# Layer 1's last norm: mean and gamma folded into the projection, squares of centered sums on ScalarE, residual added by TensorE

## The chip, the core and the metric

The kernel runs on one core of a Trainium2 chip, in one launch. The metric is the device time of that core in microseconds. Engines are named as in the profile: PE (TensorE, matmuls), DVE (VectorE), ACT (ScalarE), POOL (GpSimd) and SP (which issues the DMAs).

## The reference, cut to what matters

The input is 8 images of 192 channels and 56 x 56 pixels, in fp32. Four layers follow each other, each added to its input after a group norm. Layer 0 is an involution; layers 1 to 3 are state-space (Mamba) layers. The change is in layer 1 alone:

```python
xn = _ln(xf, ln_gamma, ln_beta)                                    # over 192 channels
xs = three slices of 64 channels, handled as three sequences
y  = _mamba(xs, ...) + skip_scale * xs
y  = y put together to 192 channels
y  = _ln(y, ln_gamma, ln_beta)                                     # the last norm
y  = y @ proj_W.T + proj_b
x  = x + y
# _ln: mu = mean(x); xc = x - mu; var = mean(xc * xc); xc * rsqrt(var + 1e-5) * g + b
```

## The kernel before

**Chunks and units.** The 3136 pixels of an image are cut into 7 chunks of 448 columns (`T`), so layer 1 has 56 chunks. A chunk is three jobs, one for each slice of 64 channels (kinds 0, 1, 2). A job is 16 units: 4 blocks of 128 inner channels times 4 groups of state rows (`nd` = 4, `NQ` = 4). The first `ssm_layer` loop runs over all units, in an order written out by hand (`manual_schedule`): each engine executes its instructions in the program's order.

**A unit** has two scans on DVE (L796), one for each half of a tile `uhg` of 128 x 4 x 448. A scan reads its decay factors from the PSUM tile `da` of that half, which ACT fills with two exponentials (`decays`, L764) as soon as the unit before has finished its scan of the same half. The scan's input is a product (L792 on DVE with a row that TensorE spread over the partitions, L752; or L785 on POOL), made one unit ahead by DVE and two ahead by POOL. After the scans ACT keeps the last column (L800, `carry`); POOL multiplies `uhg` by a row of C two units later (`readout`, L805); TensorE adds up over the states three units later (`reduce`, L814, with L811 at the start of a block); DVE multiplies the finished block by its gate (`gated`, L830). Tile `uhg` has 9 buffers. `nothing` (L820) issues matmuls with a zero weight to TensorE where the plan has little for it.

**Background steps.** All other work is made of `Step`s: matmuls, and a rest that another engine does with their result. `Steps.run` first flushes the pending rests down to `left`, then issues the step's matmuls and leaves its rest pending. So a rest is issued when a later step's `left` asks for it; `pause` (left 9) flushes nothing, `flushed` (left 0) flushes all. Matmul results lie in the PSUM pool `mm`, which has two buffers. A job has 32 places, two for a unit: an even place lies before the unit's first scan, an odd one between the first and the second. `places` deals the steps of a stretch out over its places by their costs.

**The last norm of a chunk** (`finish`) runs while the next chunk's kind-0 job is scanned, in places 18 to 31 (units 9 to 15), ahead of four gate matmul steps (L1098). It consists of `layer_norm_steps` on the tile `y` of 64 x 3 x 448:

- average: three matmuls with the constant matrix `lavg` (all 1/192), L557; its rest subtracts the mean on DVE (L563) and squares on ACT (L565, tile `sq`);
- variance: three matmuls of `lavg` with the squares, L557; its rest is logarithm and exponential on ACT (L569, L570);
- scale on DVE (L574), then the affine step on ACT, three activations (L579).

Then come two projections of three matmuls each (L1060) with a rest on DVE that adds bias and residual (L1066), and the leave step: a DMA of the chunk to the stream in HBM and two batch statistics on DVE (L298). On an image's last chunk two small group norm steps follow. In a chunk that is not an image's last, the planner puts the average at place 18, its flush at 19, the variance at 21, its flush at 22, the scale at 23, the affine step at 24, the projections at 25 and 27, and the leave step at 29. On an image's last chunk leave is at 28.

The first norm of the following chunk uses the same `layer_norm_steps` and is not changed. Weights of a layer are loaded by `load_weights` at the layer's start. In the profile an fp32 matmul shows as two records.

Of the kernel before, what the change touches and what calls it, by code (L numbers as in the profile page):

```python
# [10 lines left out]
F32 = mybir.dt.float32  # L11
BF16 = mybir.dt.bfloat16
AF = mybir.ActivationFunctionType
ALU = mybir.AluOpType
# [4 lines left out]
CP = 96  # L19
# [67 lines left out]
def conv_mamba_stack(ctx: ExitStack, tc: tile.TileContext, a, out):  # L87
# [9 lines left out]
    def const(shape, src=None, eng=None, dt=F32):  # L97
        n_const[0] += 1
        t = cst.tile(shape, dt, tag=f"k{n_const[0]}", name=f"k{n_const[0]}")
        if src is not None:  # L100
            (eng or nc.sync).dma_start(out=t, in_=src)
        return t

    def mm_tile():
        return banks.mm.tile([128, 512], F32, tag="mm", name="mm")
# [83 lines left out]
    g64 = const([64, 3], per_channel("L1_gamma", 64))  # L189
    b64 = const([64, 3], per_channel("L1_beta", 64))  # L190
    skip = const([64, 1], a["L1_skip"].partition_broadcast(64))
    skip_d = const([64, 64])
    nc.vector.tensor_scalar_mul(skip_d, ident[:64, :64], skip[:, 0:1])

# [51 lines left out]
    def load_weights(pool, w):  # L246

        pre, nd = w.pre, w.nd

        def load(tag, shape, src, eng=nc.sync):  # L250
            t = pool.tile(shape, F32, tag=tag, name=tag)
            eng.dma_start(out=t, in_=src)
            return t


        w.xproj = pool.tile([128, nd, w.rank + 2 * NS], F32, tag="w_x", name="w_x")
        xproj = a[pre + "x_proj"].rearrange("(j p) m -> p j m", p=128)
        nc.sync.dma_start(out=w.xproj[:, :, : 2 * NS], in_=xproj[:, :, w.rank :])
        nc.sync.dma_start(out=w.xproj[:, :, 2 * NS :], in_=xproj[:, :, : w.rank])
        w.dtw = pool.tile([2 * NS + w.rank, nd * 128], F32, tag="w_dt", name="w_dt")  # L260
        nc.vector.memset(w.dtw[: 2 * NS], 0.0)
        nc.sync.dma_start(out=w.dtw[2 * NS :], in_=a[pre + "dt_proj"])
        if nd == 4:
            w.inb = None
            w.outw = load("w_out", [128, 4, 64], a[pre + "out_proj"].rearrange("(j p) m -> p j m", p=128))
            w.projw = load("w_proj", [64, 3, CH], a[pre + "proj"].rearrange("(i p) o -> p i o", p=64))
        else:
            w.inw = load("w_in", [CP, NCT, 768], a[pre + "in_proj"].rearrange("(t p) m -> p t m", p=CP))
            w.inb = None
            if pre == "L2_":  # L270
                merge_embedding(pool, w)
            w.outw = load("w_out", [128, 3, CH], a[pre + "out_proj"].rearrange("(j p) m -> p j m", p=128))
            w.convd = pool.tile([128, nd, 4, 128], F32, tag="w_conv", name="w_conv")
            for j in range(nd):
                for k in range(4):
                    nc.vector.tensor_scalar_mul(w.convd[:, j, k, :], ident, w.convw[:, j, k : k + 1])
        w.dd = pool.tile([128, nd, 128], F32, tag="w_d", name="w_d")
        for j in range(nd):
            nc.vector.tensor_scalar_mul(w.dd[:, j, :], ident, w.dvec[:, j : j + 1])
# [739 lines left out]
    def mamba_jobs(pool, w):  # L1019
        jobs = []  # L1020
        chunks = Chunks(pool, 1)
        cks = chunks.all
        for ck in cks:
            c = ck.c

            def norm(c=c, ck=ck):
                def gnorm():
                    ck.xn = chunks.normalized(ck, None, 1)

                def slices():  # L1030

                    xn = ck.xn
                    xs = pool.tile([128, 3, T + 3], F32, tag="xs", name="xs", bufs=2)
                    ck.xs = xs
                    if c == 0:
                        nc.gpsimd.memset(xs[:64, :, 0:2], 0.0)
                        nc.gpsimd.memset(xs[64:, :, 0:3], 0.0)
                    else:
                        before = cks[ck.place - 1].xs
                        nc.scalar.copy(xs[:64, :, 0:2], before[:64, :, T : T + 2])  # L1040
                        nc.scalar.copy(xs[64:, :, 0:3], before[64:, :, T : T + 3])
                    for h in range(2):
                        for p0, p1, i, src in ((0, 64, 0, xn[0:64, 0, :]), (0, 32, 1, xn[64:96, 0, :]),
                                               (32, 64, 1, xn[0:32, 1, :]), (0, 64, 2, xn[32:96, 1, :])):
                            nc.sync.dma_start(out=xs[64 * h + p0 : 64 * h + p1, i, 2 + h : T + 2 + h], in_=src)

                return (
                    [Step(None, gnorm, 2)] + layer_norm_steps(pool, lambda: ck.xn, CP, NCT, g96, b96)
                    + [Step(None, slices, 2)]
                )  # L1050

            ck.norm = norm

            def finish(c=c, ck=ck):
                pps = {}

                def proj(t):
                    pps[t] = mm_tile()
                    for i in range(3):
                        nc.tensor.matmul(  # L1060
                            pps[t][:CP, :T], lhsT=w.projw[:, i, t * CP : (t + 1) * CP], rhs=ck.y[:, i, :],
                            start=(i == 0), stop=(i == 2),
                        )

                def add(t):
                    nc.vector.scalar_tensor_tensor(  # L1066
                        ck.x[:, t, :], pps[t][:CP, :T], w.projb[:, t : t + 1], ck.x[:, t, :], ALU.add, ALU.add
                    )

                return layer_norm_steps(pool, lambda: ck.y, 64, 3, g64, b64) + [  # L1070
                    Step(lambda t=t: proj(t), lambda t=t: add(t), 1, 3) for t in range(NCT)
                ] + [pause()] + chunks.leave_steps(ck)

            for i in range(3):

                def prepare(u, *beside, i=i, ck=ck, norm=norm):
                    def conv_mm(j):
                        pm = mm_tile()
                        for k in range(2):
                            nc.tensor.matmul(  # L1080
                                pm[:, :T], lhsT=w.inconv[:, k, j * 128 : (j + 1) * 128],
                                rhs=ck.xs[:, i, 2 - 2 * k : 2 - 2 * k + T], start=(k == 0), stop=(k == 1),
                            )
                        return pm

                    convs, *others, stores = project_steps(pool, w, u, conv_mm, 2, *beside)
                    if i == 0:
                        stores = stores + [Step(None, lambda: chunks.fetch_next(ck), 2)]
                        if ck.place == 0:
                            convs = norm() + convs  # L1090
                    return convs, *others, stores

                def gates(u, i=i, ck=ck):
                    normed = cks[ck.place + 1].norm() if i == 2 and ck.place + 1 < len(cks) else []

                    def z_mm(j):
                        pm = mm_tile()
                        nc.tensor.matmul(  # L1098
                            pm[:, :T], lhsT=w.inz[:, j * 128 : (j + 1) * 128], rhs=ck.xs[:64, i, 2 : T + 2], start=True, stop=True
                        )  # L1100
                        return pm

                    return normed + gate_steps(pool, w, u, z_mm, 1)

                def after(u, i=i, ck=ck, finish=finish):
                    def out_proj():
                        u.ps = mm_tile()
                        nc.tensor.matmul(u.ps[:64, :T], lhsT=skip_d, rhs=ck.xs[:64, i, 2 : T + 2], start=True, stop=False)
                        for j in range(4):
                            nc.tensor.matmul(u.ps[:64, :T], lhsT=w.outw[:, j, :], rhs=u.zs[:, j, :], start=False, stop=(j == 3))  # L1110

                    def leave():
                        if i == 0:
                            ck.y = pool.tile([64, 3, T], F32, tag="y", name="y")
                        nc.scalar.copy(ck.y[:, i, :], u.ps[:64, :T])

                    def fetch():
                        if i == 2:
                            chunks.fetch_again(ck)

                    return fetch, [Step(out_proj, leave, 1, 5)], finish() if i == 2 else []

                jobs.append((i, c == 0, prepare, gates, after))
        return jobs
# [165 lines left out]
```

## Time and profile before

| | us |
|---|---|
| median of 3 runs | 24391.19 (24375.81 to 24401.58) |
| the profiled execution | 24428.22 |
| its span | 24426.4 |
| first scan of layer 1 starts | 1623.88 |
| first scan of layer 2 starts | 16705.70 |
| mean granted TensorE clock | 0.84 |

The page gives each engine's busy time and share of the span. The groups give, after the count, busy microseconds in all and mean nanoseconds of one, and then the idle time of the engine just before them. The timeline gives start, length, engine, line and operation; a bracket names the idle time before it and what ended it. Durations of neighbours on an engine overlap a little, so that start to start is shorter than a duration.

### The profile page before, as it was taken

The page shows a single profiled execution, that of the slowest core. Times are in us where ns is not written, and L with a number is a line of the kernel's source. Part 1 is how long each engine was busy: PE and PEld are TensorE (multiplying, and loading weights), DVE is VectorE, ACT ScalarE, POOL GpSimd, SP SyncE. Part 2 cuts the span into 40 slices and gives each one's busy share as a digit, 9 for nine tenths or more (in the row PEclk, how much of TensorE's full clock was granted, in tenths as well). Part 3 has the DMA queues.
Part 4 walks back from the last instruction along what each step waited for, and adds up shares of the span by engine and source line. Part 5 has one row for each costly group of instructions (what it writes and reads, how often), then busy time and mean ns, then how long its engine had stood idle before and what let it go on. Part 6 is the DMA issues. An engine that isn't in the chain of part 4 may idle for free.

```text
span 24426.4 us, 238439 instructions
## 1 busy us (share of the span) xinstructions
PE 20547.5 (84%) x74445; PEld 6487.3 (27%) x74445; DVE 23026.9 (94%) x15882; ACT 17006.8 (70%) x32578; POOL 22738.4 (93%) x6775
## 2 busy tenths in 40 slices
PE   8988888888888888888888888888888887888888
PEld 2222222222222222222222222222333332333332
DVE  8989999999999999999999999997999998999999
ACT  2137777777777777777777777776777776777777
POOL 5669999999999999999999999997999998999999
PEclk9987888878887887887887887878989898999998
DMA  4433333333333333333333333333444443444443
GB/s 111 109 106 131 128 126 133 127 127 130 132 128 126 131 128 125 132 130 125 130 128 126 130 130 128 128 129 111 140 141 142 141 139 123 142 144 144 142 143 129
DMA packets 1209092, 3171.55 MB, mean 130 GB/s; under 512 B 166444, under 2 KB 470596, under 8 KB 1207688
## 3 DMA queue, kind: packets, MB, share of 16 engines
q1 hardware_dynamic: 1205016, 3155.25, 39.4%
q8 instruction: 584, 9.57, 0.2%
q14 instruction: 692, 5.67, 0.1%
q10 hardware_dynamic: 2800, 1.06, 0.0%
HBM read 2438.45 MB, written 555.55 MB: 123 GB/s over the span
## 4 chain that ended last, share of the span: by engine, by line
DVE 35%; PE 29%; ACT 14%; issue 11%; POOL 6%; DMA 5%; SPq 1%; DVEq 0%; POOLq 0%; ACTq 0%
DVE uhg L796 22%; DVE uhg L792 8%; ACT da L764 6%; PE y L814 4%; POOL uhg L805 4%; DMA rows<-bc 3%; PE mm L1110 3%; PE mm L1168 3%; PE mm L655 2%; PE mm L1080 2%; PE mm L621 2%; POOL uhg L785 2%; PE mm L429 2%; ACT dt L663 1%; PE y L820 1%
## 5 line engine op out<-in xcount | busy, mean ns | idle before, releaser
L796 DVE TENSOR_TENSOR_SCAN uhg<-da,uhg 128x898 f32<-128x898 f32 x8064 | 15913.4, 2011 | 606.9 <-ACT da L764 586.1
L805 POOL TENSOR_TENSOR uhg<-uhg,rows 128x1792 f32<-128x1792 f32 x4032 | 14730.5, 3674 | 283.6 <-ACT carry L800 267.4
L764 ACT ACTIVATE da<-rep,k 128x448 f32<-128x448 f32 x16128 | 10262.3, 636 | 1436.8 <-DVE uhg L796 1064.1
L785 POOL TENSOR_TENSOR uhg<-rep,rows 128x1792 f32<-128x1792 f32 x1795 | 7160.6, 3989 | 784.6 <-DMA rows<-bc 435.6
L814 PE MATMUL y<-uhg,k 128*32 128x448 f32 x32256 | 4516.4, 634 | 343.1 <-POOL uhg L805 341.4
L792 DVE TENSOR_TENSOR uhg<-rep,b 128x1792 f32<-128x1792 f32 x2237 | 4469.6, 1998 | 180.2 <-PE b L752 132.4
L800 ACT COPY carry<-uhg 128x4 f32<-128x4 f32 x4032 | 784.5, 195 | 3506.5 <-DVE uhg L796 3427.8
L820 PE MATMUL y<-w_d,k 128*128 128x448 f32 (+1 forms) x5280 | 2490.5, 575 | 0.0
L811 PE MATMUL y<-xc,w_d 128*128 128x448 f32 x2016 | 1533.4, 856 | 1091.2 <-DVE zs L830 1091.1
L1098 PE MATMUL mm<-xs,k 64*128 64x448 f32 x1344 | 875.4, 755 | 773.5 <-ACT zs L694 587.5
L655 PE MATMUL mm<-dbl,w_dt 36*128 36x448 f32 (+1 forms) x2016 | 1319.6, 753 | 222.4 <-ACT k L637 222.4
L814 PEld LDWEIGHTS y<-uhg,k 128*32 128x32 f32 x32256 | 679.9, 114 | 3093.6 <-issue 1935.2
L820 PEld LDWEIGHTS y<-w_d,k 128*128 128x128 f32 x5280 | 1023.1, 210 | 1645.0 <-issue 1618.3
L1136 PE MATMUL mm<-v,w_in 96*128 96x448 f32 x2688 | 1284.0, 612 | 80.3 <-ACT zs L696 36.8
L752 PE MATMUL b<-k,k 96*128 96x448 bf16 x2237 | 852.2, 381 | 446.5 <-DVE uhg L792 446.3
L1080 PE MATMUL mm<-xs,k 128*128 128x448 f32 x2688 | 1155.1, 571 | 26.3 <-ACT zs L694 11.3
L667 PE MATMUL mm<-xc,k 128*128 128x448 f32 x2016 | 1033.1, 630 | 84.4 <-DVE dt L670 84.4
L1168 PE MATMUL mm<-xin,w_conv 128*128 128x448 f32 x2688 | 1088.6, 547 | 1.4 <-ACT xin L696 0.8
L441 DVE TENSOR_TENSOR prod<-mm,shifted 128x448 f32<-128x448 f32 x1680 | 930.0, 613 | 152.5 <-PE mm L429 77.0
L811 PEld LDWEIGHTS y<-xc,w_d 128*128 128x128 f32 x2016 | 470.7, 270 | 1941.0 <-DVE zs L830 1375.2
L449 POOL TENSOR_TENSOR x<-x,one 96x448 f32<-96x448 f32 x560 | 630.7, 1134 | 265.3 <-DVE one L441 247.8
L621 PE MATMUL mm<-xc,w_x 128*36 128x448 f32 (+1 forms) x2016 | 816.4, 546 | 10.5 <-ACT xc L616 10.5
(138 smaller groups left out, 19388.1 us busy)
## 6 DMA issues: line engine op xcount, KB each, us to landing
rep<-ops SPq DMA_DIRECT2D x4032, 448.0 KB, 5.8
ops<-dt SPq DMA_DIRECT2D x1008, 448.0 KB, 3.2
rows<-bc SPq DMA_DIRECT2D x1960, 224.0 KB, 6.3
shifted<-xpad SPq DMA_DIRECT2D x672, 179.0 KB, 4.5
xg<-stream SPq DMA_DIRECT2D x168, 336.0 KB, 7.7
xr<-stream SPq DMA_DIRECT2D x168, 336.0 KB, 7.0
stream<-xr SPq DMA_DIRECT2D x112, 336.0 KB, 7.5
xs<-xg SPq DMA_DIRECT2D x224, 112.0 KB, 2.3
```

The costliest lines, as they stand in the source:

```text
L621: nc.tensor.matmul(u.ps[:nk, :T], lhsT=w.xproj[:, j, :], rhs=u.xc[:, j, :], start=(j == 0), stop=(j == nd - 1))
L655: nc.tensor.matmul(u.dps[j][:, :T], lhsT=w.dtw[:, j * 128 : (j + 1) * 128], rhs=u.dbl[:nk, :], start=True, stop=True)
L764: nc.scalar.activation(t[:, 64 + 449 * r : 512 + 449 * r], reps[k // NQ][:, 2 * h + r, 0, :], AF.Exp, scale=w.neg_a[:, j * NR + 2 * h + r, ...
L785: nc.gpsimd.tensor_mul(uhg[k][:, :, 1:], reps[k // NQ][:, :, 1, :], b)
L792: nc.vector.tensor_mul(uhg[k][:, :, 1:], reps[k // NQ][:, :, 1, :], b)
L796: nc.vector.tensor_tensor_scan(v, banks.da[h][:, 63:961], v, 0.0, ALU.mult, ALU.add)
L805: nc.gpsimd.tensor_mul(v, v, us[i].rows[1, q].unsqueeze(1).to_broadcast([128, NR, T]))
L811: nc.tensor.matmul(ys[k // NQ][:, :T], lhsT=w.dd[:, j, :], rhs=us[i].xc[:, j, :], start=True, stop=False)
L814: nc.tensor.matmul(y[32 * r : 32 * r + 32, :T], lhsT=fold, rhs=uhg[k][:, r, 1:], start=False, stop=(q == NQ - 1))
L820: nc.tensor.matmul(ys[k // NQ][:, : nd * 112], lhsT=zeros, rhs=w.dd.rearrange("p j e -> p (j e)")[:, : nd * 112], start=False, stop=False,)
L1080: nc.tensor.matmul(pm[:, :T], lhsT=w.inconv[:, k, j * 128 : (j + 1) * 128], rhs=ck.xs[:, i, 2 - 2 * k : 2 - 2 * k + T], start=(k == 0), st ...
L1168: nc.tensor.matmul(pm[:, :T], lhsT=w.convd[:, j, k, :], rhs=ck.xin[:, j, k : k + T], start=(k == 0), stop=(k == 3))
```

## The change

The mean and gamma are folded into the projection's weights when layer 1's weights are loaded (beta into the projection's bias). The variance's squares no longer come from a centered `y`: TensorE makes the centered slice `y_i - mean` in PSUM, three matmuls for each slice, and ACT squares it from there. The scale multiplies the uncentered `y`. The affine step is gone. Each projection has a fourth matmul, the identity times the residual, and its rest is an ACT activation with the bias instead of an add on DVE.

```diff
@@ constants
+    centers = const([64, 2, 64])
+    nc.vector.tensor_scalar_mul(centers[:, 1, :], lavg[:64, :64], -1.0)
+    nc.vector.tensor_add(centers[:, 0, :], ident[:64, :64], centers[:, 1, :])
@@ load_weights, layer 1
+            for t in range(NCT):
+                pm = mm_tile()
+                for i in range(3):
+                    nc.tensor.matmul(
+                        pm[:CP, :1], lhsT=w.projw[:, i, t * CP : (t + 1) * CP], rhs=b64[:, i : i + 1],
+                        start=(i == 0), stop=(i == 2),
+                    )
+                nc.vector.tensor_add(w.projb[:, t : t + 1], w.projb[:, t : t + 1], pm[:CP, :1])
+            for i in range(3):
+                nc.vector.tensor_scalar_mul(w.projw[:, i, :], w.projw[:, i, :], g64[:, i : i + 1])
+            pm = mm_tile()
+            for i in range(3):
+                nc.tensor.matmul(pm[:64, :CH], lhsT=lavg[:64, :64], rhs=w.projw[:, i, :], start=(i == 0), stop=(i == 2))
+            for i in range(3):
+                nc.vector.tensor_sub(w.projw[:, i, :], w.projw[:, i, :], pm[:64, :CH])
@@ finish
                 def proj(t):
                     pps[t] = mm_tile()
+                    nc.tensor.matmul(pps[t][:CP, :T], lhsT=ident[:CP, :CP], rhs=ck.x[:, t, :], start=True, stop=False)
                     for i in range(3):
                         nc.tensor.matmul(
                             pps[t][:CP, :T], lhsT=w.projw[:, i, t * CP : (t + 1) * CP], rhs=ck.y[:, i, :],
-                            start=(i == 0), stop=(i == 2),
+                            start=False, stop=(i == 2),
                         )
 
-                def add(t):
-                    nc.vector.scalar_tensor_tensor(
-                        ck.x[:, t, :], pps[t][:CP, :T], w.projb[:, t : t + 1], ck.x[:, t, :], ALU.add, ALU.add
-                    )
-
-                return layer_norm_steps(pool, lambda: ck.y, 64, 3, g64, b64) + [
-                    Step(lambda t=t: proj(t), lambda t=t: add(t), 1, 3) for t in range(NCT)
-                ] + [pause()] + chunks.leave_steps(ck)
+                def out(t):
+                    nc.scalar.activation(ck.x[:, t, :], pps[t][:CP, :T], AF.Identity, bias=w.projb[:, t : t + 1])
+
+                st = {}
+
+                def centered(i):
+                    st[i] = mm_tile()
+                    for k in range(3):
+                        nc.tensor.matmul(
+                            st[i][:64, :T], lhsT=centers[:, int(k != i), :], rhs=ck.y[:, k, :], start=(k == 0), stop=(k == 2)
+                        )
+
+                def square(i):
+                    if i == 0:
+                        st["sq"] = pool.tile([CP, 3, T], F32, tag="sq", name="sq")
+                    nc.scalar.activation(st["sq"][:64, i, :], st[i][:64, :T], AF.Square)
+
+                def variance():
+                    st["ps"] = mm_tile()
+                    for i in range(3):
+                        nc.tensor.matmul(
+                            st["ps"][:64, :T], lhsT=lavg[:64, :64], rhs=st["sq"][:64, i, :], start=(i == 0), stop=(i == 2)
+                        )
+
+                def rstd():
+                    pv = st["ps"]
+                    nc.scalar.activation(pv[:64, :T], pv[:64, :T], AF.Ln, bias=eps[:64, :])
+                    nc.scalar.activation(pv[:64, :T], pv[:64, :T], AF.Exp, scale=-0.5)
+
+                def scale():
+                    nc.vector.tensor_mul(ck.y, ck.y, st["ps"][:64, :T].unsqueeze(1).to_broadcast([64, 3, T]))
+
+                return [Step(lambda i=i: centered(i), lambda i=i: square(i), min(i, 1), 3) for i in range(3)] + [
+                    pause(1.0), Step(variance, rstd, 0, 3), flushed(), pause(), Step(None, scale, 0), pause(1.5),
+                ] + [Step(lambda t=t: proj(t), lambda t=t: out(t), 1, 4) for t in range(NCT)] + [pause()] + chunks.leave_steps(ck)
```

## The prediction

> **What bounds the kernel now.** I read the page first, for the engines and the chain that ended last.
>
> ```profile
> PE 20547.5 (84%) x74445; PEld 6487.3 (27%) x74445; DVE 23026.9 (94%) x15882; ACT 17006.8 (70%) x32578; POOL 22738.4 (93%) x6775
> DVE 35%; PE 29%; ACT 14%; issue 11%; POOL 6%; DMA 5%; SPq 1%; DVEq 0%; POOLq 0%; ACTq 0%
> ```
>
> VectorE and GpSimd are both nearly full, so the whole-span shares do not tell which one a saved microsecond helps. The busy time by stretch does, for layer 1 alone (columns as in the header: stretch, length, then PE, PEld, DVE, ACT, POOL busy, granted clock).
>
> ```profile
> 1700.00:16600.00 14900.00, 12429.28 (x40027) 3645.85 (x40026) 14292.43 (x8623) 10859.33 (x20855) 14568.15 (x3916) 0.80 0.38 128
> ```
>
> A chunk takes 266.24 us (the norm's scaling L574 starts at 8365.95, 8632.20 and 8898.43), so 14900 us are 56 chunks. DVE idles 608 us there, 10.9 a chunk; POOL 332, 5.9 a chunk. POOL is the fuller one, but its products lie some 10 us ahead of the scans that read them, and DVE's waits for POOL are 11 us in all. DVE's own order, with its waits for ACT and PE, sets the pace; POOL leaves room for at most 5.9 us a chunk. Next the groups of the last norm, one chunk's DVE and ACT in order of time, and the granted clock there.
>
> ```profile
> L579 ACT ACTIVATE y<-y,k,k 64x448 f32<-64x448 f32 x165 | 112.7, 746 | 0.0
> L574 DVE TENSOR_TENSOR y<-y,mm 64x1344 f32<-64x1344 f32 x55 | 84.7, 1540 | 0.0
> L563 DVE TENSOR_TENSOR y<-y,mm 64x1344 f32<-64x1344 f32 x55 | 83.6, 1521 | 0.0
> ```
>
> ```profile
> 8354.37 1.52 DVE L563 TENSOR_TENSOR y<-y,mm 64x1344 f32<-64x1344 f32 x1
> 8355.82 5.85 DVE L796 TENSOR_TENSOR_SCAN uhg<-da,uhg 128x898 f32<-128x898 f32 x3
> ...
> 8365.95 1.54 DVE L574 TENSOR_TENSOR y<-y,mm 64x1344 f32<-64x1344 f32 x1
> 8367.42 5.85 DVE L796 TENSOR_TENSOR_SCAN uhg<-da,uhg 128x898 f32<-128x898 f32 x3
> 8374.21 2.03 DVE L796 TENSOR_TENSOR_SCAN uhg<-da,uhg 128x898 f32<-128x898 f32 x1 [0.94 <-ACT da L764]
> ...
> 8381.92 1.25 DVE L1066 SCALAR_TENSOR_TENSOR xr<-mm,k,xr 96x448 f32<-96x448 f32 x2
> 8383.09 1.14 DVE L298 BATCH_NORM_STATS2 stats<-xr 96x6 f32<-96x448 f32 x2
> 8384.15 2.00 DVE L796 TENSOR_TENSOR_SCAN uhg<-da,uhg 128x898 f32<-128x898 f32 x1
> ```
>
> ```profile
> 8370.86 2.05 ACT L579 ACTIVATE y<-y,k,k 64x448 f32<-64x448 f32 x3
> 8372.82 1.29 ACT L764 ACTIVATE da<-rep,k 128x448 f32<-128x448 f32 x2
> ...
> 8382.04 1.31 ACT L764 ACTIVATE da<-rep,k 128x448 f32<-128x448 f32 x2 [0.46 <-DVE uhg L796]
> ```
>
> ```profile
> 8354.80:8358.30 3.50, 1.34 (x7) 0.45 (x4) 3.50 (x3) 2.85 (x6) 3.50 (x2) 1.00 0.00 0
> 8358.30:8361.70 3.40, 2.82 (x4) 0.45 (x2) 3.40 (x3) 2.33 (x5) 3.40 (x2) 0.50 0.00 0
> 8361.70:8365.10 3.40, 2.87 (x10) 0.70 (x10) 3.40 (x3) 3.25 (x7) 3.40 (x1) 0.50 0.18 55
> 8365.10:8368.50 3.40, 3.40 (x8) 1.33 (x5) 3.40 (x3) 0.48 (x2) 3.40 (x2) 0.50 0.93 289
> ```
>
> To be seen: DVE has no idle here but one gap, 0.94 us at 8374.21. It is caused by the three affine activations, which stand in ACT's queue ahead of the decays of that scan. And TensorE runs at half clock from 8358.3 to 8368.5, just where the variance matmuls lie; the granted clock shows the same dip at this place (mean 0.54 to 0.60 over the two units) in the other chunks.
>
> **Per chunk, along DVE.** I write the gain as a minus.
>
> Centering removed from DVE: from its start to the next scan's, 8354.37 to 8355.82, −1.45 us. The three center-and-sum products go to TensorE; nothing on DVE waits for them directly.
>
> Affine removed from ACT: the gap behind it, −0.94 us. The squares are cut in three; 448 columns read from PSUM cost ACT about 0.6 us (the Identity with bias of the same kind, L660, shows 625 ns), so no block of 2 us stands before a decay any more.
>
> Residual and bias moved off DVE: the two adds were 1.17 us (8381.92 to 8383.09). But both results stay pending until the leave step, which flushes them and queues the two statistics right behind. The statistics now wait for ACT, and ACT first runs the two decays that the scan just ended has released (8382.04, 1.24 to the next issue), a copy (0.08) and then the evictions at 0.6 each. First statistics 8384.05, second 8384.6, next scan 8385.15 instead of 8384.15: +1.0 us. Behind the waiting statistics stand the next scan and all of DVE. On images' last chunks the step falls before the other scan of the unit, with the same ACT work ahead.
>
> Scale waiting for the variance: the planner's costs put the steps, in half-unit places, as sums at 18, 19 and 20, variance at 22, its flush at 23, scale at 24; before it was average 18, variance 21, flush 22, scale 23. There is no flush between the last sum and the variance, so squares 1 and 2 enter ACT's queue together with the variance step, behind the decays of unit 11. Following the queues from 8352.45 with the rows above: scan(10,1) starts 8358.2 (the centering is gone), its decays leave ACT free at 8361.6, squares 1 and 2 end at 8362.75, variance starts 8362.8. An fp32 matmul is two records (L1060 has 672 for 336), issued 0.375 us apart at full and 0.75 at half clock; three matmuls need 2.5 us to their end at full clock (average, 8350.95, 2.47) and about 4.7 at half. Logarithm and exponential take 1.15 us. At full clock the scale may begin at 8366.55 against 8366.37 when DVE gets to it: +0.2 us. If the third sum (free to start at 8358.35, when square 0 has left its bank) and the variance both run at half clock, square 2 waits for the sum until 8363.5, the variance ends 8368.1, and the scale waits until 8369.3: +2.9 us. Between these ends I take the middle, +1.55: the clock row speaks for half speed, but the extra sums fill part of the idle stretch (PE busy 1.34 of 3.50 us) ahead of the dip.
>
> Sum: −1.45 − 0.94 + 1.0 + 1.55 = +0.16 us a chunk, times 56 = +9 us.
>
> [...]
>
> TensorE gains 8 matmuls a chunk, 16 records of 0.375, 6 us, and loses three filler matmuls of unit 11 (2.25 us). I cost these at nothing beyond the wait above: in the same stretch it idles 2.15, 1.11, 0.99, 0.74 and 3.19 us, the products' row spread (L752) is read 5 us or more after it, and the gate matmul, which waits for the adds now (3.19), will wait 1.5 us longer for the evictions but end before ACT's next gate copy. Without that cover it is up to 6 us a chunk.
>
> Once only: the folding at the start of layer 1. DVE there idles 9.45 us before the first norm; 12 small records (0.22 each by the 24 of L229 in 5.28 us), 6 of 192 columns and eight short DVE operations put about 3 us before the first average; bounds 0 and 6. The very last norm runs uncovered, three sums instead of one against no centering: +1, bounds 0 and 4. Two 64x64 operations among the constants: nothing.
>
> The profiled execution took 24428.22 us, 37 above the median of 24391.19. On it the sum is 24428 + 13; carried to the median, 24391 + 9 + 3 + 1 = 24404 us.
>
> **One thing that holds the time where it is.** The granted clock changes at multiples of 3.413 us, and a regular chunk of 266.24 us is 78.00 of them; seven chunks with an image's end (7502.20 to 9376.09) are 549.0. The chunk time is locked to these windows: an earlier or later DVE meets TensorE at another phase and is partly given back at its next waits for PE. This speaks for a result near zero.
>
> **Rivals.**
>
> Full clock: the sums keep TensorE busy enough and the stall is 0.2. Then −1.19 a chunk, −67 + 4: 24328 us. For it: of the clock's windows of 3.413 us in layer 1 that PE filled at full clock, 1370 of 1420 were followed by another at full clock. Against: the idle before the third sum remains, some 1.8 us.
>
> Half clock, the slow side: third sum and variance both at half clock, the stall on DVE before the scale is 2.9 us, +1.51 a chunk, +85 + 4: 24480 us. From a stall of 1.4 us on a chunk is slower, from 2.2 by over 0.2%. For it: the dip is there in all chunks at this place. Against: the third sum fills the first half-clock window, which may end the dip earlier.
>
> The whole relief arrives, 1.45 + 1.17 + 0.94 = 3.56 a chunk: 24391 − 199 + 4 = 24196. It needs statistics that don't wait for ACT; the queue order speaks against it.
>
> TensorE becomes the bound, 6 us a chunk on the path: 24391 + 336 + 4 = 24731. Its idle times speak against it.
>
> **Numbers.** Likeliest, near 24404: 0.40. Full clock 0.23, whole relief 0.03: faster by over 0.2% 0.26 (0.2%, 49 us, is about what a measurement of this kernel can tell from no change). Half clock 0.29, TensorE bound 0.05: slower 0.34. The range takes in full and half clock with the bounds of the start: 24315 to 24490.
>
> **What would show it.** No DVE group of 64x1344 but the scale, x56; the scan's gap behind the affine gone; statistics idle about 2 us before them in each chunk, ended by ACT's eviction; scale idle 0 to 2.9 us before it, ended by the exponential; the granted clock near the variance deciding which. I am wrong if the statistics don't wait, if the scale waits 4 us or more, or if scans elsewhere in the chunk lose time to TensorE.

## The result and the profile after

The change makes the kernel slower: 24549.43 us (median of 4 runs, 24546.11 to 24575.99) against 24392.60 (4 runs, 24375.81 to 24401.58), ratio 1.0068, 95% interval 1.0055 to 1.008. That is 157 us, or 2.80 us for each of layer 1's 56 chunks. The forecast was 24404 and the range ended at 24490.

The profiled execution took 24546.41 us, of which the span is 24544.6. The first lines of its page, engines and chain:

```profile
PE 20830.5 (85%) x75029; PEld 6555.6 (27%) x75029; DVE 22892.8 (93%) x15724; ACT 16989.3 (69%) x32634; POOL 22748.3 (93%) x6775
DVE 35%; PE 32%; ACT 12%; issue 11%; DMA 5%; POOL 5%; SPq 1%; DVEq 0%; POOLq 0%; ACTq 0%
```

DVE lost 134 us of work, and the time grew all the same; TensorE's share of the chain rose from 29 to 32%. The same 14900 us of layer 1 as before (length, then PE, PEld, DVE, ACT, POOL busy, granted clock):

```profile
1700.00:16600.00 14900.00, 12632.39 (x40202) 3683.21 (x40200) 14037.83 (x8382) 10764.85 (x20755) 14437.47 (x3879) 0.80 0.38 127
```

DVE now idles 862 us there instead of 608, and POOL 463 instead of 332: both wait more, so it is not the work of either that grew into the bound. The groups of DVE in layer 1 of after show where. Line numbers are 18 higher than before up to the first loop and 46 higher at the gate matmuls: L670 has become L688, L764 L782, L796 L814, L667 L685, L820 L838. The idle time is at the end of each line.

```profile
L688 DVE TENSOR_TENSOR dt<-dt,mm 128x448 f32<-128x448 f32 x664 | 391.1, 611 | 200.1 <-ACT da L782 169.9 <-PE mm L685 11.8 <-ACT carry L818 3.6
L1114 DVE TENSOR_TENSOR y<-y,mm 64x1344 f32<-64x1344 f32 x55 | 85.0, 1546 | 122.1 <-ACT mm L1111 122.1
L316 DVE BATCH_NORM_STATS2 stats<-xr 96x6 f32<-96x448 f32 x110 | 63.2, 614 | 111.5 <-ACT xr L1085 111.5
```

Two of the three waits were forecast: the scale waits 2.2 us for the exponential, the first statistics 2.0 us for ACT's eviction, in the mean of 55 chunks. The largest was not. It lies outside the last norm, at the products dt x x (L688), dt times x, which prepare the next job's scans; in before they waited 32.6 us in all:

```profile
L670 DVE TENSOR_TENSOR dt<-dt,mm 128x448 f32<-128x448 f32 x664 | 381.3, 608 | 32.6 <-ACT da L764 18.2 <-PE mm L667 7.9 <-ACT carry L800 3.6
```

The last norm of the same chunk as in the prediction, DVE and then ACT in order of time (after):

```profile
8416.50 1.55 DVE L1114 TENSOR_TENSOR y<-y,mm 64x1344 f32<-64x1344 f32 x1 [2.24 <-ACT mm L1111]
8417.97 5.85 DVE L814 TENSOR_TENSOR_SCAN uhg<-da,uhg 128x898 f32<-128x898 f32 x3
8423.75 1.99 DVE L810 TENSOR_TENSOR uhg<-rep,b 128x1792 f32<-128x1792 f32 x1
8425.66 3.93 DVE L814 TENSOR_TENSOR_SCAN uhg<-da,uhg 128x898 f32<-128x898 f32 x2
8431.61 1.15 DVE L316 BATCH_NORM_STATS2 stats<-xr 96x6 f32<-96x448 f32 x2 [2.02 <-ACT xr L1085]
```

```profile
8410.85 0.54 ACT L1099 ACTIVATE sq<-mm 64x448 f32<-64x448 f32 x1 [0.93 <-PE mm L1092]
...
8415.33 0.59 ACT L1110 ACTIVATE mm<-mm,k 64x448 f32<-64x448 f32 x1 [2.63 <-PE mm L1104]
...
8429.63 1.31 ACT L782 ACTIVATE da<-rep,k 128x448 f32<-128x448 f32 x2 [0.46 <-DVE uhg L814]
8430.87 0.18 ACT L790 COPY uhg<-carry 128x4 f32<-128x4 f32 x1
8430.95 1.15 ACT L1085 ACTIVATE xr<-mm,k 96x448 f32<-96x448 f32 x2
```

The third square waits for the third sum and the logarithm for the variance, both on TensorE. TensorE was at half clock through all of it, and busy (after, columns as above):

```profile
8405.90:8419.50 13.60, 13.42 (x27) 3.47 (x31) 11.36 (x8) 7.56 (x17) 13.60 (x5) 0.50 0.49 171
```

Now the third wait, in the following job, some 65 us after the statistics. DVE and then TensorE of after:

```profile
8489.53 1.99 DVE L810 TENSOR_TENSOR uhg<-rep,b 128x1792 f32<-128x1792 f32 x1
8491.44 2.02 DVE L814 TENSOR_TENSOR_SCAN uhg<-da,uhg 128x898 f32<-128x898 f32 x1
8497.15 1.32 DVE L688 TENSOR_TENSOR dt<-dt,mm 128x448 f32<-128x448 f32 x2 [3.69 <-ACT da L782]
```

```profile
8490.81 4.41 PE L838 MATMUL y<-w_d,k 128*128 128x448 f32 x6
8495.15 0.96 PE L832 MATMUL y<-uhg,k 128*32 128x448 f32 x8
8496.04 1.77 PE L685 MATMUL mm<-xc,k 128*128 128x448 f32 x4
```

The bracket names ACT's decays, but the bracket shows an inferred releaser; the product also reads the matmul L685, which starts at 8496.04, and its `dt` was written by an activation that ended at 8493.72. The last to come was TensorE's matmul. Ahead of it stand six records of the fillers (L838), at half clock 4.41 us long. The same place in before:

```profile
8440.01 2.52 PE L820 MATMUL y<-w_d,k 128*128 128x448 f32 x6
8442.47 0.96 PE L814 MATMUL y<-uhg,k 128*32 128x448 f32 x8
8443.36 1.77 PE L667 MATMUL mm<-xc,k 128*128 128x448 f32 x4
```

```profile
8445.32 1.13 DVE L670 TENSOR_TENSOR dt<-dt,mm 128x448 f32<-128x448 f32 x2
```

There the clock had come back before the fillers. The two stretches, before and then after, by clock:

```profile
8426.50:8436.80 10.30, 8.93 (x17) 1.91 (x17) 10.30 (x7) 7.70 (x17) 10.30 (x4) 0.50 0.41 131
8436.80:8453.80 17.00, 11.86 (x50) 4.05 (x46) 16.25 (x13) 14.05 (x25) 17.00 (x6) 1.00 0.34 137
```

```profile
8474.10:8484.40 10.30, 8.47 (x17) 1.91 (x17) 10.30 (x7) 7.70 (x17) 10.30 (x4) 0.50 0.37 113
8484.40:8494.60 10.20, 10.20 (x25) 3.16 (x19) 9.06 (x5) 8.58 (x13) 10.20 (x4) 0.50 0.17 66
8494.60:8504.80 10.20, 6.74 (x29) 2.15 (x27) 7.22 (x8) 5.27 (x13) 7.45 (x3) 1.00 0.44 180
```

Before, half clock lasted three windows of 3.413 us from 8426.5; after, six from 8474.1. From here on a chunk's 48 units are counted through its three jobs, 0 to 47; the last norm of the chunk before runs in units 9 to 15, the wait at dt x x lies in unit 25. Half clock begins in unit 22. Counted from that unit's first scan (8425.58 and 8473.64), TensorE's records agree for the first 9.8 us. After that one kernel has its clock back and the other not, though in the second of after's three lines TensorE is busy 10.20 us of 10.20.

A regular chunk (no image's end near it) now takes 269.65 us, 79.00 windows, where it took 78.00. Where the microseconds lie, by the starts of scans, median of 32 chunks of before and 29 of after (those with the long half clock):

| units | before, us | after, us | difference |
|---|---|---|---|
| 9 to 15 (the last norm) | 39.92 | 40.70 | +0.78 |
| 20 and 21 | 10.54 | 10.07 | −0.47 |
| 22 to 26 | 27.05 | 30.73 | +3.68 |
| 36 to 39 | 20.25 | 19.90 | −0.35 |
| the others | 168.48 | 168.25 | −0.23 |
| a chunk | 266.24 | 269.65 | +3.41 |

What the norm loses, 0.78, is more than given back elsewhere; the loss is in units 22 to 26. Six windows of half clock stand there in 46 of after's 56 chunks and in 6 of before's. 40 more times 3.68 are 147 us; from the first scan of layer 1 to that of layer 2 the two profiled executions differ by 142.8 us (15081.8 and 15224.6), the medians of the whole by 157.

**Three theories**, to which the expectations below refer by letter. A: the new waits shift DVE's order against the clock's windows, half clock then lasts longer around units 22 to 26, and the chunk locks to the next whole window; without the filler matmuls or at another phase the loss is gone. B: the loss is DVE's delay itself, each microsecond of the new waits with what follows it, whatever TensorE's fillers do. C: the loss is TensorE's work, eight matmuls more in a chunk.

### The profile page after: what moved, and what is told of

It reads as the page before. It is cut to its first block, busy times and chain, and to the rows that moved or that the text cites. A ratio compares the mean times of both kernels' runs of the same rounds, so it can differ in the third digit from the quotient of the medians.

```text
span 24544.6 us, 239417 instructions
## 1 busy us (share of the span) xinstructions
PE 20830.5 (85%) x75029; PEld 6555.6 (27%) x75029; DVE 22892.8 (93%) x15724; ACT 16989.3 (69%) x32634; POOL 22748.3 (93%) x6775
## 4 chain that ended last, share of the span: by engine, by line
DVE 35%; PE 32%; ACT 12%; issue 11%; DMA 5%; POOL 5%; SPq 1%; DVEq 0%; POOLq 0%; ACTq 0%
DVE uhg L814 23%; DVE uhg L810 8%; ACT da L782 5%; PE y L832 5%; DMA rows<-bc 4%; POOL uhg L823 3%; PE mm L673 3%; PE mm L1156 2%; PE y L838 2%; PE mm L1214 2%; PE mm L685 2%; PE mm L639 2%; PE mm L1126 2%; PE mm L447 1%; PE y L829 1%
## 5 line engine op out<-in xcount | busy, mean ns | idle before, releaser
L814 DVE TENSOR_TENSOR_SCAN uhg<-da,uhg 128x898 f32<-128x898 f32 x8064 | 15898.5, 2009 | 546.2 <-ACT da L782 537.3
L782 ACT ACTIVATE da<-rep,k 128x448 f32<-128x448 f32 x16128 | 10261.8, 636 | 1608.3 <-DVE uhg L814 1243.4
L838 PE MATMUL y<-w_d,k 128*128 128x448 f32 (+1 forms) x4950 | 2361.6, 580 | 0.0
L1144 PE MATMUL mm<-xs,k 64*128 64x448 f32 x1344 | 814.7, 705 | 848.9 <-ACT zs L712 652.6
L838 PEld LDWEIGHTS y<-w_d,k 128*128 128x128 f32 x4950 | 966.1, 212 | 1568.8 <-issue 1543.7
L685 PE MATMUL mm<-xc,k 128*128 128x448 f32 x2016 | 1027.6, 627 | 90.4 <-DVE dt L688 89.7
L688 DVE TENSOR_TENSOR dt<-dt,mm 128x448 f32<-128x448 f32 x1008 | 590.1, 608 | 328.9 <-ACT da L782 169.9
```

Source lines behind the costliest of these rows:

```text
L685: nc.tensor.matmul(u.xps[j][:, :T], lhsT=ident, rhs=u.xc[:, j, :], start=True, stop=True)
L782: nc.scalar.activation(t[:, 64 + 449 * r : 512 + 449 * r], reps[k // NQ][:, 2 * h + r, 0, :], AF.Exp, scale=w.neg_a[:, j * NR + 2 * h + r, ...
L814: nc.vector.tensor_tensor_scan(v, banks.da[h][:, 63:961], v, 0.0, ALU.mult, ALU.add)
L838: nc.tensor.matmul(ys[k // NQ][:, : nd * 112], lhsT=zeros, rhs=w.dd.rearrange("p j e -> p (j e)")[:, : nd * 112], start=False, stop=False,)
```

## The experiments

Each is timed against the kernel before on the same chip (medians of before there: 24389.38 for the first four, 24387.72 for the next four, 24395.19 for the last four). Chunk lengths, stretches of units and phases are worked out from the starts of scans and the clock's changes in the trace.

**The residual back on DVE** (change of after):

```diff
-                    nc.tensor.matmul(pps[t][:CP, :T], lhsT=ident[:CP, :CP], rhs=ck.x[:, t, :], start=True, stop=False)
...
-                            start=False, stop=(i == 2),
+                            start=(i == 0), stop=(i == 2),
...
-                    nc.scalar.activation(ck.x[:, t, :], pps[t][:CP, :T], AF.Identity, bias=w.projb[:, t : t + 1])
+                    nc.vector.scalar_tensor_tensor(
+                        ck.x[:, t, :], pps[t][:CP, :T], w.projb[:, t : t + 1], ck.x[:, t, :], ALU.add, ALU.add
+                    )
```

> The changed kernel with its residual part undone: projections of three matmuls, bias and residual added on VectorE, planner costs left as changed. Theory A (lock to the clock's windows): the change cost VectorE only about +0.75 us a chunk in units 9 to 14 (+2.2 wait of the scale, +0.94 statistics, -1.45 centering, -0.94 affine gap); the other 2.7 us come from units 22 to 26, where the half-clock stretch lasts 6 windows of 3.413 us and not 3, so that a regular chunk locks to 79 windows (269.65) and not 78 (266.24). With the adds back the local sum is about -0.2, the chunk goes back to 78 windows and the time to 24390 +- 30. Theory B (the waits themselves are the loss): 24549 - 56 x (1.73 - 1.17), about 24518. Theory C (8 more matmuls on TensorE are the loss): 2 of 8 taken away, 24510.

Measured: 24379.62 us, ratio 0.9995 (0.9986 to 1.0005). Undoing this one part undoes the whole loss. The scale still waits 124.7 us in layer 1. Some chunks take 78.0 windows each; most alternate between 267.9 and 264.5 us, two together 156.0 windows. A's number holds; B and C put it over 24500.

**The residual's part alone** (change of before: the same edit the other way round).

> The kernel before with the residual part alone: identity matmul with the residual in each projection, bias by ScalarE, planner costs as before. Theory A: +0.94 us a chunk on VectorE is more than the lock at 78 windows can take in (the slope of chunk time against phase gives room for some 0.3 us), so chunks of 79 windows: about 24555; or, if it is not locked, +53 us. Theory B: the statistics wait 2 us, the adds' 1.17 are gone: +50 us, 24440. Theory C: 2 of 8 matmuls, +40 us, 24430.

Measured: 24552.78 us, 1.0064 (1.0049 to 1.0079), the time of the full change. Chunks take 79 windows; the waits of the statistics for ACT and of dt x x are both there, though nothing of the norm's sums was touched (us in all, times, longest):

```profile
DVE dt L670 <- ACT da L764: 157.2, 43, 3.7
DVE stats L298 <- ACT xr L1067: 129.7, 66, 2.4
```

The 43 are the 43 chunks with six windows. B (24440) and C (24430) are missed. So this part alone brings the whole loss; the rest of the change comes out near nothing, by −1.45 and −0.94 against 2.24 of waiting at the scale.

**A delay on DVE** (change of before): two statistics of 448 columns repeated in each chunk, 1.07 us.

```diff
                     add_stats(ck.stats, ck.c, ck.x)
+                    if self.layer == 1:
+                        for t in range(2):
+                            nc.vector.bn_stats(ck.stats[:, t, ck.c, :], ck.x[:, t, :])
```

> The kernel before with two statistics of layer 1's leave step made twice on VectorE (same values again): 1.07 us more VectorE work a chunk and nothing else. Theory A: the answer is a step, not a line: 78 windows (about 24392) or 79 (about 24555). Theories B and C: 56 x 1.07 = +60 us, 24452, in chunks of 267.3 us.

Measured: 24516.46 us, 1.0048 (1.0032 to 1.0065). 1.07 x 56 is 60 us, measured are 127 (24516.46 − 24389.38): the delay is doubled. Regular chunks are a mixture of 78.3 to 79.2 windows, and the wait at dt x x is there (144.0 us in all). Neither the clean step of A nor a simple sum; with no matmul added C can't explain it.

**After without the three filler matmuls of unit 24** (the six records of L838 shown above):

```diff
             more = 3 - math.ceil(load_of(plan[2 * m] + plan[2 * m + 1]))
+            if nd == 4 and jobs[i][0] == 1 and m == 8:
+                more = 0
```

> The changed kernel without the three filler matmuls of unit 8 in jobs of kind 1 (a chunk's unit 24), which took 4.3 us at half clock right before the matmuls that VectorE waits for in unit 25. Theory A: the wait of 3.7 us in unit 25 shrinks to 0.5 or less, the chunk falls to 78 windows or below: 24350 to 24410. Theories B and C: the loss lies in units 9 to 14, the time stays at 24549 +- 25.

Measured: 24392.37 us, 1.0001 (0.9992 to 1.001). The groups of DVE in layer 1 (line numbers 2 higher):

```profile
L688 DVE TENSOR_TENSOR dt<-dt,mm 128x448 f32<-128x448 f32 x664 | 380.9, 608 | 14.1 <-PE mm L685 6.4 <-ACT dt L681 2.4 <-issue 0.2
L1116 DVE TENSOR_TENSOR y<-y,mm 64x1344 f32<-64x1344 f32 x56 | 86.6, 1546 | 138.1 <-ACT mm L1113 138.1
L316 DVE BATCH_NORM_STATS2 stats<-xr 96x6 f32<-96x448 f32 x111 | 63.8, 615 | 116.2 <-ACT xr L1087 116.2
```

Both forecast waits are as long as in after, and the 157 us are gone with the third alone. This decides against B, which leaves the fillers out of it. Chunks take 78 windows: units 9 to 15 take 40.70 us as in after, units 22 to 26 27.05 as in before, and the 0.78 is given back in the other units. One thing is to be noted: half clock lasts three windows in 53 of the 56 chunks, beginning 0.54 us after unit 22's first scan. So leaving the fillers out did not make six windows cheap, it left almost none; why is not shown. What six windows cost without them can be read in the 3 chunks left, 28.17 us in units 22 to 26.

**Before without the same fillers**, as a control.

> The kernel before without the three filler matmuls of unit 8 in jobs of kind 1. Theory A: VectorE waits only 0.33 + 0.66 us a chunk there before, so at most 1 us is to be had, and the lock at 78 windows may keep it: 24340 to 24395. If fillers there are useless work in general (theory C), the same.

Measured: 24394.80 us, 1.0004 (0.9995 to 1.0013). Leaving the fillers out is worth nothing by itself, so the gain in the run above is not theirs.

**Eight more matmuls in before**, as dummies ahead of the projections:

```diff
                     pps[t] = mm_tile()
+                    for again in range(4):
+                        nc.tensor.matmul(
+                            pps[t][:CP, :T], lhsT=w.projw[:, 0, t * CP : (t + 1) * CP], rhs=ck.y[:, 0, :], start=True, stop=True
+                        )
```

> The kernel before with eight more matmuls a chunk on TensorE: each of the two projections first makes its first product four times over (overwritten afterwards), planner costs as before. Nothing on VectorE or ScalarE is changed. Theory C (TensorE's added work is the loss): 24549. Theory A (phase against the clock's windows): the matmuls stand where TensorE idled 3.2 us before the gates, VectorE is moved by less than 0.5 us, chunks stay at 78 windows: 24392 +- 25, unless the shifted gate matmuls alone tip it to 79 (24555). Theory B: 24392.

Measured: 24772.32 us, 1.0163 (1.0146 to 1.018). All three numbers are missed (A and B 24392, C 24549). The run is not a clean test of C: in one bunch ahead of the adds the matmuls hold up the adds directly, 298.5 us in layer 1 (DVE's wait for L1064). What it shows is a warning: matmuls just ahead of a result that DVE waits for are on the path.

**The steps moved** (change of after; all eight extra matmuls stay): the scale goes from place 24 to 25, so that the variance is nearly done, and the evictions are flushed at 28, one place ahead of the statistics.

```diff
-                return [Step(lambda i=i: centered(i), lambda i=i: square(i), min(i, 1), 3) for i in range(3)] + [
-                    pause(1.0), Step(variance, rstd, 0, 3), flushed(), pause(), Step(None, scale, 0), pause(1.5),
-                ] + [Step(lambda t=t: proj(t), lambda t=t: out(t), 1, 4) for t in range(NCT)] + [pause()] + chunks.leave_steps(ck)
+                return [Step(lambda i=i: centered(i), lambda i=i: square(i), min(i, 1), 2.5) for i in range(3)] + [
+                    pause(0.2), Step(variance, rstd, 0, 3), flushed(), pause(1.5), Step(None, scale, 0), pause(0.2),
+                ] + [Step(lambda t=t: proj(t), lambda t=t: out(t), 1, 2.5) for t in range(NCT)] + [
+                    pause(0.5), flushed(0.5), pause(0.5),
+                ] + chunks.leave_steps(ck)
```

> The changed kernel with its two waits mended and the fillers kept: other costs and pauses, so that the scale lies one place later (25 instead of 24 in most chunks) and a flush step puts the projection's evictions on ScalarE half a unit before the leave step (28, 29). VectorE's local sum is then about -1.45 - 0.94 - 1.17 + 0.3 = -3.3 us a chunk against before. Theory B: 24392 - 183 = 24210. Theory A: a multiple of half a window a chunk: 78 (24392), 77.5 (24300) or 77 (24200), depending on where the half-clock stretch of units 22 to 25 falls.

Measured: 24233.01 us (24231.62 to 24265.65), 0.9937 (0.9923 to 0.9952): faster than both kernels, by 155 us than before and, by medians of separate measurements, by 316 than after. Chunks take 77.00 windows. Its groups of DVE and its stretch of layer 1:

```profile
L688 DVE TENSOR_TENSOR dt<-dt,mm 128x448 f32<-128x448 f32 x670 | 385.5, 608 | 67.7 <-ACT dt L681 30.7 <-ACT carry L818 21.5 <-PE mm L685 3.9
L1114 DVE TENSOR_TENSOR y<-y,mm 64x1344 f32<-64x1344 f32 x56 | 86.6, 1546 | 43.6 <-ACT mm L1111 43.6
L316 DVE BATCH_NORM_STATS2 stats<-xr 96x6 f32<-96x448 f32 x112 | 69.5, 621 | 45.5 <-ACT xr L1085 39.1
```

```profile
1700.00:16600.00 14900.00, 12725.61 (x40935) 3730.25 (x40936) 14214.44 (x8528) 10898.46 (x21028) 14608.48 (x3930) 0.81 0.38 129
```

The scale's wait falls from 122.1 to 43.6 us and the statistics' from 111.5 to 45.5. The matmuls are all there and the time is 0.6% below before: C falls here. A and B are not told apart by this run: units 9 to 15 take 37.17 us, 2.75 less than before, and 2.75 x 56 = 154 us is what was gained, whether or not a lock is at work.

**The same without the fillers.**

> The mended kernel also without the three fillers of unit 8 in jobs of kind 1. Theory A: without them a long half-clock stretch costs VectorE nothing in unit 25, so the -3.3 us arrive more fully: 77 windows, 24200 +- 40. Theory B: as the mended kernel with fillers.

Measured: 24245.12 us, 0.9939 (0.9924 to 0.9954). At 77 windows the fillers make no difference that shows.

**The delayed kernel without the fillers** (the two repeated statistics and `more = 0`).

> The kernel before with the same 1.07 us of extra VectorE statistics a chunk that cost 124 us, now without the three fillers of unit 8 in jobs of kind 1. Theory A (the loss beyond the local sum is made in units 24 and 25, by fillers at half clock): at most the plain sum, 56 x 1.07 = +60, and back to 78 windows where the lock holds: 24392 to 24452. Theory B (a delay costs what it costs, wherever): 24516 again.

Measured: 24474.34 us, 1.003 (1.0019 to 1.0042). The loss falls from 127 to 79 us, but not to A's number: two chunks take 157 windows, 78.5 each. Without fillers six windows of half clock still cost about 1 us in units 22 to 26 (28.2 us against 27.1), and 25 of the 56 chunks have them. So the fillers are a part of the loss, some 48 of 127 us here, and A gets the size wrong by 22 us or more; B's 24516 is missed as well.

**Only the evictions earlier** (change of after: scale at 24 as there, evictions flushed at 28), and **only the scale later** (scale at 25, evictions with leave as there):

```diff
+                    pause(0.2), Step(variance, rstd, 0, 3), flushed(), pause(1.0), Step(None, scale, 0), pause(1.5),
+                ] + [Step(lambda t=t: proj(t), lambda t=t: out(t), 1, 3) for t in range(NCT)] + [
+                    pause(0.2), flushed(0.5), pause(1.0),
+                ] + chunks.leave_steps(ck)
```

> The changed kernel with one of the two mends: a flush step puts the projection's evictions half a unit before the leave step (28, 29); scale and variance stay at their places. Local sum on VectorE against before: +0.75 - 0.94 - 1.17 = -1.4 us a chunk. Theory A: back to 78 windows, 24392 +- 25, or 77.5, 24300; the full 1.4 us would be 24314. Theory B: 24549 - 56 x 2.1 = 24431.

```diff
+                    pause(0.2), Step(variance, rstd, 0, 3), flushed(), pause(2.0), Step(None, scale, 0), pause(0.5),
+                ] + [Step(lambda t=t: proj(t), lambda t=t: out(t), 1, 3) for t in range(NCT)] + [
+                    pause(1.0), pause(1.0),
+                ] + chunks.leave_steps(ck)
```

> The changed kernel with the other mend alone: the scale one place later (25), the evictions still flushed with the leave step. Local sum: +0.75 - 2.0 = -1.25 us a chunk. Theory A: 78 windows, 24392 +- 25, or 77.5, 24300. Theory B: 24549 - 56 x 2.0 = 24437.

Measured: 24365.46 (0.9989, 0.9979 to 0.9998) and 24350.01 us (0.9982, 0.9972 to 0.9991). The waits part as intended: with early evictions 135.4 us at the scale and 23.7 at the statistics, with the late scale 40.7 and 121.9. Either alone takes away the loss of after, 184 and 199 us, and gains only 30 and 45 on before; both together gain 155. Units 9 to 15 take 38.81 and 38.74 us, 1.11 and 1.18 less than before, which would be 62 and 66 us in all; a part is given back. The chunks stay near 78 windows with the first and mix 77.3 to 78.0 with the second.

**Half the delay** (change of before: one repeated statistics, 0.53 us a chunk).

> The kernel before with one of the two statistics made twice, 0.53 us more VectorE work a chunk. Theory A: not the plain +30 us (24422), but chunks of 78 or 79 windows or a mix of them: near 24392 or above 24450. Theory B: 24422.

Measured: 24378.32 us, 0.9995 (0.9986 to 1.0004). Added work on DVE that costs nothing: 0.53 us x 56 would be 30 us. With delays of 0, 0.53 and 1.07 us the kernel takes 24392, 24378 and 24516, which is no straight line. Units 9 to 15 take 40.67 us here, 0.75 more than before, all of it given back; half clock begins 0.56 us after unit 22's first scan and lasts three windows.

**Phase and length.** In all these traces, 784 chunks, the half-clock stretch around unit 22 goes by when it begins, counted from that unit's first scan:

| half clock begins, us | lasts, windows | units 22 to 26, us | kernels, with the number of their 56 chunks |
|---|---|---|---|
| −1.71 to 0.20 | 4 | 27.1 to 27.6 | residual on DVE 33, delay of 1.07 us 18, that delay without fillers 25; 0 to 7 in the others |
| 0.27 to 0.55 | 6 | 30.6 to 30.7; 28.2 without fillers | after 46, residual alone 43, delay of 1.07 us 31, that delay without fillers 25, eight more matmuls 31, residual on DVE 17; 0 to 7 in the others, mostly in an image's first chunk (before 6) |
| 0.53 to 3.48 | 3 | 27.0 to 27.6 | before 47, half delay 53, after without fillers 53, before without fillers 48, steps moved 49 in both runs, early evictions 54, late scale 47; 6 to 20 in the others |

In regular chunks the usual beginning is 0.53 us in after, 0.46 with the residual alone, 0.96 in before, 0.54 in after without fillers, 0.56 with half the delay. After has six windows up to 0.546 and three from 0.552. The border is not the same in all kernels: after without fillers has six at 0.529 and three from 0.539, and in the delayed kernel without fillers both stand at 0.533. What is shown by this: units 22 to 26 take 3.6 to 3.7 us longer with six windows where the fillers are there, in every kernel, and a few hundredths of a microsecond of phase go with six or three. A long chunk does not follow everywhere. In the run with the residual on DVE the wait of 3.67 us at dt x x lies in chunks that take 268.6 us from scale to scale, and those between take 263.9 to 264.1, so that the mean stays at 78 windows. With eight more matmuls the chunks without six windows are the longer ones. Why the clock stays at half for six windows there, with the same TensorE records in the first 9.8 us, stays open; nothing was run that sets the phase alone.

## Why the prediction was wrong

**Right, term by term.** Centering off DVE −1.45; the gap behind the affine step gone; statistics held up by ACT, predicted +1.0, measured +0.94 in a regular chunk; the dip of the clock falling on the third sum and the variance; the order in each queue. The two gains and the wait of the statistics came to their predicted sum within 0.1 us.

**Mis-sized:** the scale's wait. "Between these ends I take the middle, +1.55"; it was 2.2. The clock row had spoken for half speed, and the discount for the sums that fill the idle stretch was not earned: granted clock 0.50 from 8405.9 to 8419.5. Locally a chunk is then +0.78 us instead of +0.16 (units 9 to 15), some 44 us in all; by the prediction's own sum that would have been 24439, inside the range. It did not even cost that: the run without the fillers has the same +0.78 and the time of before.

**The step that failed** is "One thing that holds the time where it is". The lock to the clock's windows was seen, and read as a spring that pulls towards 78.00 windows: "This speaks for a result near zero." The spring is there: without the fillers it gives back the norm's 0.78 us whole, with a half clock that begins 0.54 us after unit 22's first scan and no longer 0.96. The failure is that the giving back was taken to go on, while it moves the phase, and the phase has an edge where half clock changes its length. Chunks 16 to 18 of after (counted from 0), thrown off by an image's end, show the way there: half clock begins at 1.32, 0.70 and 0.55 us (0.552) and lasts three windows, and from one unit 22 to the next they take 266.9, 266.4 and 266.2 us. In chunk 19 it begins at 0.546 and lasts six, and that chunk takes 269.7. There DVE waits 3.7 us at dt x x and units 22 to 26 are 3.68 us longer; with the norm's 0.78, less 1.05 given back, that is one window, 3.41. So the next chunk meets the clock at the same place, and the lock holds at 79.00. Half the delay stays on the near side of the edge: fillers in place, +0.75 in units 9 to 15, half clock from 0.56 us, 78 windows, and no loss. Most of the window is the new wait, outside the norm, which the sum had at nothing.

**The cover that was only half checked.** "I cost these at nothing beyond the wait above": the idle times of TensorE were read in the last norm alone, at the clock of before. The matmuls that were added cost nothing themselves, as the run with the steps moved shows, whose gain is the whole of its 2.75 us a chunk; the fillers that were already there took 1.9 us more (4.41 against 2.52) once the clock was half. The closing sentence had the right sign of error in it, "if scans elsewhere in the chunk lose time to TensorE", but no rival had it priced: the slow rival ended at the local +1.51.

**The rivals.** Half clock came nearest in its stall (2.9 predicted as the end, 2.2 measured) and was 69 us short in its sum. The whole relief was called all but impossible because "the queue order speaks against it". True for the order in the change; moving two steps by a place gave most of it, 155 us, a whole window in regular chunks.

**The clock.** The granted clock changes at multiples of 3.413 us in the traces of before and of after. The prediction let the clock depend on how full TensorE is: sums that "keep TensorE busy enough", a third sum that "may end the dip earlier". That was the author's estimate, and the runs show less: three windows with 10.20 us busy of 10.20 stood at half clock throughout (8484.4 to 8494.6 above), and what brings the clock back is not shown. Two counts of the prediction come out a little otherwise by the trace of before: of layer 1's full windows at full clock some 1430 of 1475 were followed by another (97%; the prediction had 1370 of 1420), and the clock over units 10 and 11 was 0.54 to 0.71.

## What to carry to other kernels

In a steady loop, compare the loop's period with the period at which the granted clock changes, 3.413 us here, before adding up small savings: if it is a whole or half multiple, a small delay can cost nothing, or a whole step, here 3.41 us of 266. In this loop 0.75 us more in units 9 to 15 cost nothing (half the delay) and 0.78 cost 3.41 (after), or nothing without the fillers; on the other side savings of 1.1, 1.2 and 2.75 us a chunk brought 0.5, 0.8 and 2.8. Price the steps of the lock as rivals of their own, and look for the wait that would fill it in the whole iteration, not only beside the edit. When work moves to another engine, move the steps that wait for it too: the same edit was 0.7% slower with the order that it came with and 0.6% faster with two steps one place later or earlier.

## What was unexpected in the hardware

- Around unit 22 half clock lasts three, four or six windows of 3.413 us for much the same work, and in after less than 0.01 us of phase lies between six and three (0.546 and 0.552).
- A TensorE that is fully busy by the profile for three windows can stay at half clock throughout: 10.20 of 10.20 us busy at 0.50 (after, 8484.4 to 8494.6).
- Filler matmuls, there to keep TensorE busy, cost more where it is slow: six records took 2.52 us at full clock and 4.41 at half, ahead of a matmul that DVE was waiting for.
- A loop can also lock to half windows: two chunks together 157 windows in the delayed kernel without fillers.
- Work on an engine that is busy 96% of the time can cost nothing: 0.53 us a chunk more on DVE in layer 1 (14292 of 14900 us busy) left the time where it was (0.9995, 0.9986 to 1.0004).
